# Late routing of the expert stages in a fixed order, with the indices first

## The chip, the cores and the metric

The kernel runs on one core of a Trainium2 chip. The metric is the device time of one execution in microseconds (us). The core has five engines with a queue each, which run their own instructions in order and wait for one another by semaphores: TensorE (PE in the profile, with its weight loads as PEld), VectorE (DVE), ScalarE (ACT), GpSimd (POOL) and SyncE (SP). SP issues most DMA transfers, POOL the indirect ones (gathers and scatters by an index).

## The reference, cut to what matters

A graph network with four layers over 1250 tokens of 512 features. Each layer adds the output of two mixers (a graph part and an attention part), and then that of a mixture of experts:

```python
xn = _layernorm(x, axis=-1)
x = x + _L2_gnn_ref(xn, edge_index, ...) + _L2_mix_ref(xn[None], ...)[0]
x = x + _L2_ffn_ref(_layernorm(x, axis=-1)[None], ...)[0]
...
# the experts, here those of layer 3: every token goes to its 2 best of 8 experts
logits = flat @ gate_w.T
top_vals, top_idx = jax.lax.top_k(logits, TOP_K)
top_w = jax.nn.softmax(top_vals, axis=-1)
combine = jnp.sum(jax.nn.one_hot(top_idx, E, dtype=flat.dtype) * top_w[..., None], axis=1)
out = jnp.zeros_like(flat)
for e in range(E):
    hdn = jax.nn.gelu(flat @ w1[e] + b1[e])
    out = out + combine[:, e:e + 1] * (hdn @ w2[e] + b2[e])
```

The reference computes all experts for all tokens and weights them. The kernel computes only the chosen pairs.

## The kernel before, in words

Everything is float32 in the products that matter. Tokens stand in ten groups of 125. The eight stages (mixers and experts of layers 0 to 3) follow each other, written as one Python function each (L2566). A scheduler then orders the instructions of each engine: it may draw an instruction ahead of others in the program, except those that `tc.keep_in_program_order` pins, which keep their place among the pinned ones. `Pinned` (L308) is a stand-in for VectorE that pins each instruction issued through it.

In an expert stage the 2500 pairs of token and expert are packed into tiles of 128 slots (`SL`). The first three tiles (`NFIRST`) belong to experts 0, 1 and 2 with fixed numbers; they hold the first 128 pairs of each of these. All others are dynamic: tiles in pairs that share an expert (256 slots) and single ones, and the expert of each is only known when the routing has been computed. A load (`Experts.loads`) is one expert's weights with one or two tiles.

`place` (L313) is the routing. Its early part ranks every pair within its expert (products with a triangle and with ones, L327 to L332), makes `r_ohl`, the one-hot of the slot in the tile, and with a product (L373) the token numbers of the first three tiles: `r_idxf`, and `r_destf`, where their results go. `experts.first_rows` then requests the rows of the first tiles from DRAM (`xg<-rows,r_idxf`, L505). The late part is the function `rest` (L391). It works out how many tiles each expert has, and from that the tile of each pair (`r_slot`, `r_own`, `r_slf`), its one-hot `r_oht` (L428, L429), a second product `r_oht` by `r_ohl` on TensorE (L431, 20 matmuls), from its result the token numbers of the dynamic tiles (`r_idx`, L435), the expert number of each load (`r_exi`, L437 to L450), the destinations (`r_dest`, L451) and the weights of the two choices (`shares`, L453). SP loads each expert number into a register (L483) before it can issue the DMA of that expert's weights. The gathers of dynamic rows on POOL need `r_idx`.

`Experts.each` (L519) drives the tiles: for each load n it fetches ahead (weights and rows of a later load), turns the rows of the next load (four transposes on TensorE and a copy to `xgT`, `by_feature`, L544) and yields the load to the stage's own code, which runs the expert's two or three products and scatters the result `y` to a table in DRAM (L566). In layers 0, 1 and 3 the second product's result goes through an add on VectorE (L560 in `put`). Layer 2 works in three groups of loads: `Group.first` (L2332) runs the first products of a whole group, and `second` and `third` follow later.

What the steps of the prediction touch: `rest` is called in `each` at n == 1 (L522), that is behind the code of tile 0; `turn` (L513) copies tile 0's rows on ScalarE and all others on VectorE (L517). These lines decide it:

```python
517  self.turned.append(by_feature(self.to, self.got[n][2], nc.vector.tensor_copy if n else nc.scalar.copy))
521  if n == 1:
522      self.rest()
```

Of the kernel before, what the change touches and what calls it, by code (L numbers as in the profile page):

```python
# [25 lines left out]
E = 8  # L26
# [9 lines left out]
SL = 128  # L36
# [23 lines left out]
def gps_d4_kernel(ctx: ExitStack, tc: tile.TileContext, a: dict, out: bass.AP):  # L60
# [252 lines left out]
    def place(tmp, n_, choice, experts, soft=True, aside=lambda n: None):  # L313
# [5 lines left out]
            return pool.tile(shape, dt, tag=tag, name=name, bufs=1)  # L319

        v = nc.vector
        m, oh = choice.either, choice.oh
        m1, m2 = choice.best

# [11 lines left out]
        ranks = rank[:, None, :NT, :].to_broadcast([TP, 2, NT, E])  # L336

        def size_of(o, ids):
            v.scalar_tensor_tensor(o, ids, -1.0, ids, op0=OP.mult, op1=OP.max)

        ids = sm("r_ids", [SL, NTI])
        size = sm("r_size", [SL, NTI])
# [1 line left out]
        def destination(name, at):  # L344
            w = at.stop - at.start
            kind = sm(f"{name}k", [SL, w])
            v.tensor_scalar(kind, ids[:, at], 0.0, None, op0=OP.is_lt)
            v.scalar_tensor_tensor(kind, size[:, at], 2.0, kind, op0=OP.mult, op1=OP.add)
            free = sm(f"{name}s", [SL, w])
            v.scalar_tensor_tensor(free, ids[:, at], 0.0, spare[:, at], op0=OP.is_equal, op1=OP.mult)  # L350
            dest = sm(name, [SL, w], I32)
            v.scalar_tensor_tensor(dest, kind, -2.0, free, op0=OP.add, op1=OP.add)
            return dest

        own = sm("r_own", [TP, 2, NT, E])
# [33 lines left out]
        aside(1)  # L389

        def rest():  # L391
            v.scalar_tensor_tensor(n[:, 0, :], n[:, 1, :], -2.0, n[:, 0, :], op0=OP.mult, op1=OP.add)
            pm = sm("r_pm", [TP, 2, E, E])
            v.tensor_tensor(pm, uptos, n[:, :, None, :].to_broadcast([TP, 2, E, E]), op=OP.mult)
            end = sm("r_end", [TP, 2, E])
            v.tensor_reduce(end, pm, AX.X, OP.add)
            base = sm("r_base", [TP, 1])
            v.tensor_scalar(base, end[:, 1, E - 1:E], 2.0 * NPAIR * SL, None, op0=OP.max)

            q = sm("r_q", [TP, 3, E])  # L400
            v.tensor_scalar(q[:, 1, :], n[:, 1, :], 2.0 * SL, None, op0=OP.mult)
            v.scalar_tensor_tensor(q[:, 0, :], n[:, 1, :], -2.0 * SL, end[:, 1, :], op0=OP.mult, op1=OP.add)
            v.scalar_tensor_tensor(q[:, 2, :], n[:, 0, :], -1.0 * SL, end[:, 0, :], op0=OP.mult, op1=OP.add)
            v.scalar_tensor_tensor(q[:, 2, :], q[:, 2, :], base, end[:, 1, :], op0=OP.add, op1=OP.subtract)
# [5 lines left out]
            v.tensor_tensor(single, kept[:, :NT, :], q_(1), op=OP.is_ge)  # L410
            slot = sm("r_slot", [TP, NT, E])
            v.tensor_tensor(slot, kept[:, :NT, :], q_(0), op=OP.add)
            late = sm("r_late", [TP, 2, NT, E])
            v.scalar_tensor_tensor(late, kept[:, None, :NT, :].to_broadcast([TP, 2, NT, E]), 0.0, oh, op0=OP.is_ge, op1=OP.mult)
            v.tensor_tensor(single, single, q_(2), op=OP.mult)
            v.tensor_tensor(slot, slot, single, op=OP.add)
            own = sm("r_own", [TP, 2, NT, E])
            v.scalar_tensor_tensor(own, slot[:, None, :, :].to_broadcast([TP, 2, NT, E]), float(SL), late,
                                   op0=OP.add, op1=OP.mult)
            slf = sm("r_slf", [TP, 2 * NT])  # L420
            v.tensor_reduce(slf, own.rearrange("p k t e -> p (k t) e"), AX.X, OP.add)
            sl = sm("r_sl", [TP, 2 * NT], I32)
            v.tensor_copy(sl, slf)
            v.tensor_scalar(sl, sl, 7, None, op0=OP.logical_shift_right)
            slf = sm("r_slf", [TP, 2 * NT])
            v.tensor_copy(slf, sl)
            oht = sm("r_oht", [TP, 2 * NT, NREST], F16)
            v.tensor_tensor(oht, bc(slf, NREST), lanes[:, None, 1:NREST + 1].to_broadcast([TP, 2 * NT, NREST]), op=OP.is_equal)  # L428
            v.tensor_tensor(oht, oht, bc(tokid, NREST), op=OP.mult)  # L429
            ps = bank()  # L430
            mm(ps[:, :NREST], [(ohl[:, j, :], oht[:, j, :]) for j in range(2 * NT)])  # L431
            idx = sm("r_idx", [SL, NREST], I32)
            v.tensor_copy(ids[:, NFIRST:], ps[:, :NREST])
            size_of(size[:, NFIRST:], ids[:, NFIRST:])
            v.tensor_scalar(idx, size[:, NFIRST:], 1.0, 1.0, op0=OP.max, op1=OP.subtract)  # L435

            th = sm("r_th", [1, 2, E])  # L437
            v.tensor_scalar(th[:, 0, :], end[:1, 0, :], base[:1, :], None, op0=OP.add)
            v.tensor_copy(th[:, 1, :], end[:1, 1, :])
            le2 = sm("r_le2", [1, NLOAD, 2 * E])  # L440
            v.tensor_tensor(le2, bc(loadi, 2 * E), th.rearrange("p k e -> p (k e)")[:, None, :]
                            .to_broadcast([1, NLOAD, 2 * E]), op=OP.is_ge)
            ex = sm("r_ex", [1, NLOAD])
            v.tensor_reduce(ex, le2, AX.X, OP.add)
            ge = sm("r_ge", [1, NLOAD])
            v.tensor_scalar(ge, loadi, base[:1, :], -float(E), op0=OP.is_ge, op1=OP.mult)
            v.tensor_tensor(ex, ex, ge, op=OP.add)
            exi = sm("r_exi", [1, NLOAD + 1], I32)
            v.tensor_scalar(exi[:, :NLOAD], ex, float(E - 1), None, op0=OP.min)
            v.tensor_scalar(exi[:, NLOAD:], end[:1, 0, E - 1:E], base[:1, :], 1.0 / SL, op0=OP.add, op1=OP.mult)  # L450
# [7 lines left out]
    class Experts:  # L458


        def __init__(self, pool, rows, weights, rare, ahead=2, bufs=6):

            often = NLOAD - rare
            self.loads = ([(e - NFIRST, (e,)) for e in range(NFIRST)]
                          + [(i, tuple(NFIRST + t for t in tiles)) for k in range(NPAIR)
                             for i, tiles in ((k, (2 * k, 2 * k + 1)), (NPAIR + k, (2 * NPAIR + k,))) if i < often]
                          + [(k, (NFIRST + NPAIR + k,)) for k in range(2 * NPAIR, NLOAD) if k < often]
                          + [(k, (NFIRST + NPAIR + k,)) for k in range(often, NLOAD)])
            self.common = often + NPAIR
            self.often = often + NFIRST  # L470
            soon["rare"] = soon.get("rare", 0) + 1
            self.label = f"rare{soon['rare']}"
            self.pool, self.rows = pool, rows
            self.weights, self.ahead, self.bufs = weights, ahead, bufs
            self.got, self.turned = [], []
            self.ready, self.behind = [], []
            self.most = self.often
            self.fresh = lambda: None

# [15 lines left out]
        def fetch(self):  # L495
# [2 lines left out]
                return  # L498
            i, tiles = self.loads[n]
            w = self.ready[n] if n < len(self.ready) else self.weights(self.expert(i), n)  # L500
            xg = []
            for t in tiles:
                g = self.pool.tile([SL, D], F32, tag="xg", name="xg", bufs=self.bufs)
                at = self.idxf[:, t:t + 1] if t < NFIRST else self.idx[:, t - NFIRST:t - NFIRST + 1]
                nc.gpsimd.indirect_dma_start(g, None, self.rows, bass.IndirectOffsetOnAxis(ap=at, axis=0))  # L505
                xg.append(g)
            self.got.append((tiles, w, xg))

        def start(self):
            for _ in range(self.ahead):  # L510
# [1761 lines left out]
    def layer2_ffn():  # L2272
# [4 lines left out]
        with tc.tile_pool(name="l2o", bufs=1) as op, tc.tile_pool(name="l2b", bufs=1) as bp:  # L2277
# [25 lines left out]

            rows, choice = arrival[2].rows, arrival[2].end()
            experts = Experts(op, rows, weights1, 7)
            experts.fresh = lambda: (half1.fresh(), half3.fresh())
            experts.first_weights()
            place(bp, 1, choice, experts)
            with tc.tile_pool(name="l2e", bufs=1) as pool:
# [13 lines left out]
                class Group:  # L2323
# [8 lines left out]
                    def first(self, source):  # L2332
# [277 lines left out]
```

## Time and profile before

| | us |
|---|---|
| median of 3 runs (2908.19 to 2909.71) | 2908.22 |
| the profiled execution | 2900.07 |
| its span | 2898.4 |
| TensorE busy | 2699.3 (93%) |
| VectorE busy | 1540.1 (53%) |
| ScalarE busy | 787.0 (27%) |
| GpSimd busy | 630.7 (22%) |
| mean granted TensorE clock, of full | 0.966 |

The four expert stages begin, by the first gather with `r_idxf`, at 1300.96 (layer 0), 1751.04 (layer 1), 2403.29 (layer 2) and 2755.98 us (layer 3) of the span. The profiled execution is a single one, with its own time, and sums over its rows are made against that time. Idle time of an engine that nothing waits for costs nothing.

### The profile page before, as it was taken

The numbers are of one execution on the slowest core, as the hardware profiler recorded it, in microseconds if no ns is written. First come the engines' busy times: TensorE is split into PE (matmuls) and PEld (weight loads), VectorE is DVE, ScalarE is ACT, GpSimd is POOL, SyncE is SP. The second block draws the span as 40 slices with busy tenths as digits, with TensorE's granted clock in tenths as the row PEclk, the third lists the DMA queues.
The fourth block names the chain that finished last, engine by engine and source line by source line (L and its number), as shares of the span: only waits on it lengthen the run. The fifth ranks groups of instructions, "written<-read, shape, count | busy, mean of one in ns | idle before, by whom it ended". The sixth has DMA issues, their size and how long they took to land. (4 is left out here: it accounts for less than half of the span.)

```text
span 2898.4 us, 34891 instructions
## 1 busy us (share of the span) xinstructions
PE 2699.3 (93%) x12500; PEld 1924.9 (66%) x12500; DVE 1540.1 (53%) x3845; ACT 787.0 (27%) x1770; POOL 630.7 (22%) x474
## 2 busy tenths in 40 slices
PE   7999999999999999989999998999799998989984
PEld 4457778874577788755457566888654776645663
DVE  6935677674356677553635553334434376443533
ACT  3232333342333444221220452111132123421010
POOL 2444444444100110025101012111000003202141
PEclk9999999999999999999999998999899998999997
DMA  8511112221000651437650018666350016662286
GB/s 233 127 16 16 4 16 45 48 34 16 16 15 1 142 119 53 103 87 230 191 134 14 30 57 302 244 241 232 119 137 30 16 42 208 198 168 77 66 288 229
DMA packets 240092, 314.63 MB, mean 109 GB/s; under 512 B 94689, under 2 KB 136229, under 8 KB 239893
## 3 DMA queue, kind: packets, MB, share of 16 engines
q1 hardware_dynamic: 150156, 236.37, 26.9%
q0 software_dynamic: 86656, 66.90, 9.7%
q10 hardware_dynamic: 3080, 8.81, 1.0%
q8 instruction: 111, 1.82, 0.3%
q14 instruction: 89, 0.72, 0.1%
HBM read 267.80 MB, written 43.86 MB: 108 GB/s over the span
## 5 line engine op out<-in xcount | busy, mean ns | idle before, releaser
L771 POOL DMA_INDIRECT adj<-count,cell x160 | 322.7, 2017 | 375.1 <-DMA adj<-count,cell 329.9
L197 PE MATMUL ps<-xnT,w 128*128 128x500 f32 (+1 forms) x736 | 275.3, 529 | 0.6 <-DVE xnT L941 0.6
L197 PE MATMUL ps<-w,xnT 128*125 128x512 f32 x560 | 252.1, 599 | 0.6 <-ACT xnT L1837 0.6
L197 PE MATMUL ps<-xgT,w 128*128 128x256 f32 (+1 forms) x1344 | 237.0, 335 | 4.7 <-ACT xgT L551 2.1
L197 PEld LDWEIGHTS ps<-xgT,w 128*128 128x128 f32 x1344 | 212.2, 195 | 42.0 <-issue 15.4
L197 PEld LDWEIGHTS ps<-xnT,w 128*128 128x128 f32 x736 | 139.5, 193 | 122.7 <-issue 116.2
L197 PEld LDWEIGHTS ps<-w,xnT 128*125 128x125 f32 x560 | 102.3, 190 | 114.6 <-issue 113.1
L1334 PE MATMUL ps<-w,hT 128*125 128x256 f32 (+1 forms) x704 | 171.2, 379 | 0.5 <-ACT p L1339 0.5
L1339 ACT COPY p<-ps 125x256 f32<-125x256 f32 (+5 forms) x272 | 93.6, 351 | 265.5 <-PE ps L1334 245.7
L1334 PEld LDWEIGHTS ps<-w,hT 128*125 128x125 f32 (+1 forms) x704 | 130.3, 188 | 19.0 <-ACT p L1339 0.9
L551 DVE COPY xgT<-ps 128x512 f32<-128x512 f32 x90 | 59.7, 687 | 143.7 <-PE ps L550 112.5
L566 POOL DMA_INDIRECT table<-y,r_dest x82 | 85.6, 1044 | 228.8 <-DVE y L2066 124.8
L197 PE MATMUL ps<-w,hT 128*128 128x512 f32 (+1 forms) x272 | 124.7, 595 | 3.6 <-issue 2.3
L223 DVE TENSOR_TENSOR xn<-ps,xn 125x256 f32<-125x256 f32 (+1 forms) x180 | 80.2, 450 | 78.7 <-PE ps L197 54.6
L2050 ACT ACTIVATE hT<-ps,b 128x256 f32<-128x256 f32 (+1 forms) x120 | 50.5, 424 | 236.7 <-PE ps L197 225.9
L1334 PE MATMUL ps<-t,sh 128*125 128x256 f32 (+1 forms) x480 | 112.6, 379 | 0.0
L505 POOL DMA_INDIRECT xg<-rows,r_idx x82 | 79.1, 965 | 152.1 <-PE ps L550 122.5
L197 PE MATMUL ps<-hs,AT 125*125 125x512 f32 x400 | 101.6, 410 | 4.9 <-PEq L902 3.3
L1334 PEld LDWEIGHTS ps<-t,sh 128*125 128x125 f32 (+1 forms) x480 | 89.9, 188 | 12.8
L197 PE MATMUL ps<-AT,part 125*128 125x500 f32 (+1 forms) x480 | 92.6, 355 | 0.0
L197 PEld LDWEIGHTS ps<-hs,AT 125*125 125x125 f32 x400 | 75.2, 191 | 24.6 <-issue 4.6
L197 PEld LDWEIGHTS ps<-AT,part 125*128 125x128 f32 x480 | 79.3, 189 | 13.4 <-issue 1.0
(520 smaller groups left out, 5032.3 us busy)
## 6 DMA issues: line engine op xcount, KB each, us to landing
w<-in_L_ffn_we_dram SPq DMA_DIRECT2D x58, 1024.0 KB
w<-in_L_ffn_w_dram SPq DMA_DIRECT2D x62, 512.0 KB
came<-table SPq DMA_DIRECT2D x40, 448.0 KB
w<-in_L_mix_W_dram SPq DMA_DIRECT2D x16, 1024.0 KB
w<-in_L_ffn_w_dram SPq DMA_DIRECT2D x47, 256.0 KB
AT<-adj SPq DMA_DIRECT2D x10, 1093.8 KB
AT<-adj SPq DMA_DIRECT2D x20, 546.9 KB
rows<-z SPq DMA_DIRECT2D x40, 224.0 KB
```

The costliest lines, as they stand in the source:

```text
L197: nc.tensor.matmul(o, l, r, start=(i == 0), stop=(i == n - 1))
L223: nc.vector.tensor_tensor(dst, ps, dst, op=OP.add)
L505: nc.gpsimd.indirect_dma_start(g, None, self.rows, bass.IndirectOffsetOnAxis(ap=at, axis=0))
L551: copied(xgT[:, :, j * SL:(j + 1) * SL], ps.rearrange("p (c s) -> p c s", c=NC))
L566: d = nc.gpsimd.indirect_dma_start(to, bass.IndirectOffsetOnAxis(ap=at, axis=0), y, None)
L771: nc.gpsimd.indirect_dma_start(adj, bass.IndirectOffsetOnAxis(ap=self.cell[:, c:c + 1], axis=0), self.count[:, c:c + 1], None, compute_op= ...
L1334: nc.tensor.matmul(banks[b], ls(k), rs(k), start=first and k == 0, stop=k == nk - 1, skip_group_check=True)
L1339: nc.scalar.copy(o, banks[b])
L2050: nc.scalar.activation(hT[f // NC][:, f % NC, :ns], ps[:, :ns], AF.Gelu, bias=b1[:, f:f + 1])
```

## The change

`place` gets a `Pinned()` of its own, and all instructions of `rest`, `size_of` and `destination` are issued through it, so that they stand on VectorE in the order of the program, which has the indices ahead of the expert numbers and the destinations. `Experts` gets `found`, which runs `rest` and requests the rows of the first dynamic load; layer 2 calls it in its first group, behind the turning of tile 1 and ahead of tile 0's product. Where `found` ran, `each` does not call `rest` again, and `fetch` takes the rows that were asked for. In layer 2 `still` is 3, so the rows of the first three tiles are copied on ScalarE; elsewhere it is 1, as before. Layers 0, 1 and 3 call `rest` where they did.

```diff
+        pinned = Pinned()
...
         def size_of(o, ids):
-            v.scalar_tensor_tensor(o, ids, -1.0, ids, op0=OP.mult, op1=OP.max)
+            pinned.scalar_tensor_tensor(o, ids, -1.0, ids, op0=OP.mult, op1=OP.max)
...
         def rest():
-            v.scalar_tensor_tensor(n[:, 0, :], n[:, 1, :], -2.0, n[:, 0, :], op0=OP.mult, op1=OP.add)
+            pinned.scalar_tensor_tensor(n[:, 0, :], n[:, 1, :], -2.0, n[:, 0, :], op0=OP.mult, op1=OP.add)
...
-            v.tensor_tensor(oht, oht, bc(tokid, NREST), op=OP.mult)
+            pinned.tensor_tensor(oht, oht, bc(tokid, NREST), op=OP.mult)
             ps = bank()
             mm(ps[:, :NREST], [(ohl[:, j, :], oht[:, j, :]) for j in range(2 * NT)])
             idx = sm("r_idx", [SL, NREST], I32)
-            v.tensor_copy(ids[:, NFIRST:], ps[:, :NREST])
+            pinned.tensor_copy(ids[:, NFIRST:], ps[:, :NREST])
...
-            self.ready, self.behind = [], []
+            self.ready, self.behind, self.asked, self.still = [], [], {}, 1
...
             w = self.ready[n] if n < len(self.ready) else self.weights(self.expert(i), n)
+            self.got.append((tiles, w, self.asked.get(n) or self.ask(tiles)))
+
+        def ask(self, tiles):
             xg = []
             for t in tiles:
                 g = self.pool.tile([SL, D], F32, tag="xg", name="xg", bufs=self.bufs)
                 at = self.idxf[:, t:t + 1] if t < NFIRST else self.idx[:, t - NFIRST:t - NFIRST + 1]
                 nc.gpsimd.indirect_dma_start(g, None, self.rows, bass.IndirectOffsetOnAxis(ap=at, axis=0))
                 xg.append(g)
-            self.got.append((tiles, w, xg))
+            return xg
+
+        def found(self):
+
+            if not self.asked:
+                self.rest()
+                self.asked[NFIRST] = self.ask(self.loads[NFIRST][1])
...
-                self.turned.append(by_feature(self.to, self.got[n][2], nc.vector.tensor_copy if n else nc.scalar.copy))
+                self.turned.append(by_feature(self.to, self.got[n][2], nc.vector.tensor_copy if n >= self.still else nc.scalar.copy))
...
-                if n == 1:
+                if n == 1 and not self.asked:
                     self.rest()
...
+            experts.still = NFIRST
...
                             experts.turn()
+                            experts.found()
```

More of the change, by code (lines that the diff above doesn't have):

```diff
@@ L346, in destination @@
             kind = sm(f"{name}k", [SL, w])
-            v.tensor_scalar(kind, ids[:, at], 0.0, None, op0=OP.is_lt)
-            v.scalar_tensor_tensor(kind, size[:, at], 2.0, kind, op0=OP.mult, op1=OP.add)
+            pinned.tensor_scalar(kind, ids[:, at], 0.0, None, op0=OP.is_lt)
+            pinned.scalar_tensor_tensor(kind, size[:, at], 2.0, kind, op0=OP.mult, op1=OP.add)
             free = sm(f"{name}s", [SL, w])
-            v.scalar_tensor_tensor(free, ids[:, at], 0.0, spare[:, at], op0=OP.is_equal, op1=OP.mult)
+            pinned.scalar_tensor_tensor(free, ids[:, at], 0.0, spare[:, at], op0=OP.is_equal, op1=OP.mult)
             dest = sm(name, [SL, w], I32)
-            v.scalar_tensor_tensor(dest, kind, -2.0, free, op0=OP.add, op1=OP.add)
+            pinned.scalar_tensor_tensor(dest, kind, -2.0, free, op0=OP.add, op1=OP.add)
             return dest
@@ L391, in rest @@
         def rest():
-            v.scalar_tensor_tensor(n[:, 0, :], n[:, 1, :], -2.0, n[:, 0, :], op0=OP.mult, op1=OP.add)
+            pinned.scalar_tensor_tensor(n[:, 0, :], n[:, 1, :], -2.0, n[:, 0, :], op0=OP.mult, op1=OP.add)
             pm = sm("r_pm", [TP, 2, E, E])
-            v.tensor_tensor(pm, uptos, n[:, :, None, :].to_broadcast([TP, 2, E, E]), op=OP.mult)
+            pinned.tensor_tensor(pm, uptos, n[:, :, None, :].to_broadcast([TP, 2, E, E]), op=OP.mult)
             end = sm("r_end", [TP, 2, E])
-            v.tensor_reduce(end, pm, AX.X, OP.add)
+            pinned.tensor_reduce(end, pm, AX.X, OP.add)
             base = sm("r_base", [TP, 1])
-            v.tensor_scalar(base, end[:, 1, E - 1:E], 2.0 * NPAIR * SL, None, op0=OP.max)
+            pinned.tensor_scalar(base, end[:, 1, E - 1:E], 2.0 * NPAIR * SL, None, op0=OP.max)
             q = sm("r_q", [TP, 3, E])
[L401 to L404, printed above, removed]
+            pinned.tensor_scalar(q[:, 1, :], n[:, 1, :], 2.0 * SL, None, op0=OP.mult)
+            pinned.scalar_tensor_tensor(q[:, 0, :], n[:, 1, :], -2.0 * SL, end[:, 1, :], op0=OP.mult, op1=OP.add)
+            pinned.scalar_tensor_tensor(q[:, 2, :], n[:, 0, :], -1.0 * SL, end[:, 0, :], op0=OP.mult, op1=OP.add)
+            pinned.scalar_tensor_tensor(q[:, 2, :], q[:, 2, :], base, end[:, 1, :], op0=OP.add, op1=OP.subtract)
             def q_(k):
@@ L409, in rest @@
             single = sm("r_single", [TP, NT, E])
-            v.tensor_tensor(single, kept[:, :NT, :], q_(1), op=OP.is_ge)
+            pinned.tensor_tensor(single, kept[:, :NT, :], q_(1), op=OP.is_ge)
             slot = sm("r_slot", [TP, NT, E])
-            v.tensor_tensor(slot, kept[:, :NT, :], q_(0), op=OP.add)
+            pinned.tensor_tensor(slot, kept[:, :NT, :], q_(0), op=OP.add)
             late = sm("r_late", [TP, 2, NT, E])
-            v.scalar_tensor_tensor(late, kept[:, None, :NT, :].to_broadcast([TP, 2, NT, E]), 0.0, oh, op0=OP.is_ge, op1=OP.mult)
@@ L415, in rest @@
-            v.tensor_tensor(single, single, q_(2), op=OP.mult)
-            v.tensor_tensor(slot, slot, single, op=OP.add)
+            pinned.scalar_tensor_tensor(late, kept[:, None, :NT, :].to_broadcast([TP, 2, NT, E]), 0.0, oh, op0=OP.is_ge, op1=OP.mult)
+            pinned.tensor_tensor(single, single, q_(2), op=OP.mult)
+            pinned.tensor_tensor(slot, slot, single, op=OP.add)
             own = sm("r_own", [TP, 2, NT, E])
-            v.scalar_tensor_tensor(own, slot[:, None, :, :].to_broadcast([TP, 2, NT, E]), float(SL), late,
+            pinned.scalar_tensor_tensor(own, slot[:, None, :, :].to_broadcast([TP, 2, NT, E]), float(SL), late,
@@ L419, in rest @@
                                    op0=OP.add, op1=OP.mult)
             slf = sm("r_slf", [TP, 2 * NT])
-            v.tensor_reduce(slf, own.rearrange("p k t e -> p (k t) e"), AX.X, OP.add)
+            pinned.tensor_reduce(slf, own.rearrange("p k t e -> p (k t) e"), AX.X, OP.add)
             sl = sm("r_sl", [TP, 2 * NT], I32)
-            v.tensor_copy(sl, slf)
-            v.tensor_scalar(sl, sl, 7, None, op0=OP.logical_shift_right)
+            pinned.tensor_copy(sl, slf)
+            pinned.tensor_scalar(sl, sl, 7, None, op0=OP.logical_shift_right)
@@ L425, in rest @@
             slf = sm("r_slf", [TP, 2 * NT])
-            v.tensor_copy(slf, sl)
+            pinned.tensor_copy(slf, sl)
             oht = sm("r_oht", [TP, 2 * NT, NREST], F16)
-            v.tensor_tensor(oht, bc(slf, NREST), lanes[:, None, 1:NREST + 1].to_broadcast([TP, 2 * NT, NREST]), op=OP.is_equal)
-            v.tensor_tensor(oht, oht, bc(tokid, NREST), op=OP.mult)
+            pinned.tensor_tensor(oht, bc(slf, NREST), lanes[:, None, 1:NREST + 1].to_broadcast([TP, 2 * NT, NREST]), op=OP.is_equal)
@@ L432, in rest @@
             idx = sm("r_idx", [SL, NREST], I32)
-            v.tensor_copy(ids[:, NFIRST:], ps[:, :NREST])
+            pinned.tensor_copy(ids[:, NFIRST:], ps[:, :NREST])
             size_of(size[:, NFIRST:], ids[:, NFIRST:])
-            v.tensor_scalar(idx, size[:, NFIRST:], 1.0, 1.0, op0=OP.max, op1=OP.subtract)
+            pinned.tensor_scalar(idx, size[:, NFIRST:], 1.0, 1.0, op0=OP.max, op1=OP.subtract)
             th = sm("r_th", [1, 2, E])
-            v.tensor_scalar(th[:, 0, :], end[:1, 0, :], base[:1, :], None, op0=OP.add)
-            v.tensor_copy(th[:, 1, :], end[:1, 1, :])
+            pinned.tensor_scalar(th[:, 0, :], end[:1, 0, :], base[:1, :], None, op0=OP.add)
+            pinned.tensor_copy(th[:, 1, :], end[:1, 1, :])
             le2 = sm("r_le2", [1, NLOAD, 2 * E])
-            v.tensor_tensor(le2, bc(loadi, 2 * E), th.rearrange("p k e -> p (k e)")[:, None, :]
+            pinned.tensor_tensor(le2, bc(loadi, 2 * E), th.rearrange("p k e -> p (k e)")[:, None, :]
                             .to_broadcast([1, NLOAD, 2 * E]), op=OP.is_ge)
             ex = sm("r_ex", [1, NLOAD])
-            v.tensor_reduce(ex, le2, AX.X, OP.add)
+            pinned.tensor_reduce(ex, le2, AX.X, OP.add)
             ge = sm("r_ge", [1, NLOAD])
-            v.tensor_scalar(ge, loadi, base[:1, :], -float(E), op0=OP.is_ge, op1=OP.mult)
-            v.tensor_tensor(ex, ex, ge, op=OP.add)
+            pinned.tensor_scalar(ge, loadi, base[:1, :], -float(E), op0=OP.is_ge, op1=OP.mult)
+            pinned.tensor_tensor(ex, ex, ge, op=OP.add)
             exi = sm("r_exi", [1, NLOAD + 1], I32)
-            v.tensor_scalar(exi[:, :NLOAD], ex, float(E - 1), None, op0=OP.min)
-            v.tensor_scalar(exi[:, NLOAD:], end[:1, 0, E - 1:E], base[:1, :], 1.0 / SL, op0=OP.add, op1=OP.mult)
+            pinned.tensor_scalar(exi[:, :NLOAD], ex, float(E - 1), None, op0=OP.min)
+            pinned.tensor_scalar(exi[:, NLOAD:], end[:1, 0, E - 1:E], base[:1, :], 1.0 / SL, op0=OP.add, op1=OP.mult)
             soon["to"] = table[n_], destf, destination("r_dest", slice(NFIRST, NTI)), soon["to"][3]
```

## The prediction

> **What bounds the kernel now.** I read the page first.
>
> ```profile
> span 2898.4 us, 34891 instructions
> PE 2699.3 (93%) x12500; PEld 1924.9 (66%) x12500; DVE 1540.1 (53%) x3845; ACT 787.0 (27%) x1770; POOL 630.7 (22%) x474
> ```
>
> TensorE (PE) is busy 93% of the span, so what matters is whether the change opens or closes a hole on PE. The late routing runs once in each of four expert stages. I then read the timeline around each, and the table of PE's waits for the layer-1 stage from 1784 to 2045 us, which holds no row: PE has no slack there. Timeline rows are start, duration, engine, instruction, count, and in brackets the idle time before it and its releaser. Layer 1:
>
> ```profile
> 1756.35 0.72 DVE L429 TENSOR_TENSOR r_oht<-r_oht,tokid 125x540 f16<-125x540 f16 x1
> 1757.49 1.11 PE L550 MATMUL ps<-ident,xg 128*128 128x128 f32 x4 [7.35 <-DMA xg<-rows,r_idxf]
> 1759.40 10.28 PE L197 MATMUL ps<-xgT,w 128*128 128x128 f32 x64 [0.80 <-ACT xgT L551]
> 1776.82 0.66 PE L197 MATMUL ps<-r_oht,r_ohl 125*128 125x27 f16 x20
> 1777.02 0.69 DVE L560 TENSOR_TENSOR y<-ps,erow 128x512 f32<-128x512 f32 x1 [6.18 <-PE ps L197]
> 1777.33 7.39 PE L197 MATMUL ps<-xgT,w 128*128 128x128 f32 x64
> ```
>
> The reader sees that VectorE finishes `r_oht` at 1757.07, before tile 0 has even started, in time in which PE waits for rows. The routing product on PE (the fourth row) comes 20 us later and waits for nothing. The third and sixth rows are the same 64 matmuls: after the 7 us hole they took 2.89 us more. Layer 3:
>
> ```profile
> 2755.81 0.16 DVE L392 SCALAR_TENSOR_TENSOR r_n<-r_n 125x8 f32<-125x8 f32 x1
> 2760.70 0.72 DVE L429 TENSOR_TENSOR r_oht<-r_oht,tokid 125x540 f16<-125x540 f16 x1
> 2767.33 0.66 PE L197 MATMUL ps<-r_oht,r_ohl 125*128 125x27 f16 x20
> 2767.53 0.69 DVE L560 TENSOR_TENSOR y<-ps,erow 128x512 f32<-128x512 f32 x1 [1.03 <-PE ps L197]
> 2772.06 2.05 PE L197 MATMUL ps<-xgT,w 128*128 128x128 f32 x16 [0.89 <-DVE xgT L551]
> 2775.98 1.31 PE L550 MATMUL ps<-ident,xg 128*128 128x128 f32 x8 [1.00 <-DMA xg<-rows,r_idx]
> ```
>
> The same picture, with about 1.9 us of holes on PE behind it. Layer 0 and layer 2:
>
> ```profile
> 1317.01 0.66 PE L197 MATMUL ps<-r_oht,r_ohl 125*128 125x27 f16 x20
> 1317.21 0.69 DVE L560 TENSOR_TENSOR y<-ps,erow 128x512 f32<-128x512 f32 x1 [1.85 <-PE ps L197]
> 1319.50 0.99 POOL L505 DMA_INDIRECT xg<-rows,r_idx  x1 [0.30 <-DVE ws L311]
> 1325.13 2.09 PE L550 MATMUL ps<-ident,xg 128*128 128x128 f32 x8 [2.60 <-issue]
> ...
> 2408.16 1.12 PE L550 MATMUL ps<-ident,xg 128*128 128x128 f32 x4 [0.38 <-DMA xg<-rows,r_idxf]
> 2411.66 0.67 PE L197 MATMUL ps<-r_oht,r_ohl 125*128 125x27 f16 x20
> 2413.31 0.95 POOL L505 DMA_INDIRECT xg<-rows,r_idx  x1 [6.51 <-DVE r_destk L348]
> 2416.79 0.66 PE L550 MATMUL ps<-ident,xg 128*128 128x128 f32 x4 [2.25 <-DMA xg<-rows,r_idx]
> 2419.39 1.08 PE L550 MATMUL ps<-ident,xg 128*128 128x128 f32 x4 [1.95 <-DMA xg<-rows,r_idx]
> ```
>
> In layer 2 PE stands 2.25 + 1.95 = 4.2 us for the first dynamic rows.
>
> **The change, part by part.**
>
> *Fixed order, layers 0, 1, 3.* `rest()` is called at n == 1, behind tile 0's use. The scheduler had drawn its instructions ahead of that; pinned, they may not pass. In the built program VectorE's order becomes: tile 1's copy, tile 0's add `y` (L560), then the whole of `rest()`. PE's order keeps the `r_oht` product directly behind tile 0's second product and ahead of tile 1's first, and PE takes its matmuls in order. So the add waits for PE, `rest()` waits for the add, and PE waits for `rest()`: cover that was free (VectorE was idle 13 us in layer 1) is given away.
>
> Length of that wait: in layer 3 `rest()` took 2755.81 to 2761.42 = 5.61 us up to `r_oht`. Of this the eight expert-number instructions (L438 to L450), now behind the indices, held 1.48 us of start-to-start time; `r_q`, `r_single`, `r_late`, which had run earlier, add 0.51 us; some six pairs that now depend on their neighbour start about 0.12 us later each (0.16 us instructions start 0.20 apart when dependent, 0.08 when not): 5.61 - 1.48 + 0.51 + 0.7 = 5.3 us (4.6 to 5.9). The add ends 0.69 + 0.20 us after the product's old start, so PE stands 6.2 us in each of the three layers.
>
> Clock after the hole. The table of stretches (us, busy time and count of PE, PEld, DVE, ACT, POOL, then PE's granted clock, DMA share, GB/s) has, behind layer 3's hole that ended at 2759.45:
>
> ```profile
> 2760.00:2764.00 4.00, 3.33 (x16) 2.92 (x15) 1.39 (x2) 1.20 (x2) 0.00 (x0) 0.50 0.26 73
> ```
>
> PE runs there at half its clock. Restarting cost 2.89 us in layer 1 (10.28 against 7.39) and 1.74 + 0.37 = 2.1 us in layer 3 (16 matmuls 3.79 against 2.05, four transposes 0.97 against 0.60). After a 6.2 us hole I take 2.5 us in layer 1 and 2.1 in layer 3; the bounds are 0 and 3.4 us. The Trainium skill (TensorE: Matmul & The Clock Gate, section What's actually happening) says that one idle window of about 3.4 us halves the clock and that one busy window restores it; by that alone a restart would lose an estimated 1.7 us, and my total would be about 1 us lower. The row's 2.89 us is more than one such window, so the measurement decides.
>
> - Layer 1: no slack, 6.2 + 2.5 = **+8.7** (6.2 to 9.6). Its next dynamic weights are issued at 1781.26, when tile 1 frees a buffer, which moves too; the later expert numbers (about 1786) cost nothing more.
> - Layer 3: 6.2 + 2.1 - 1.9 of old holes, which the stall swallows, = **+6.4** (4.3 to 9). The rows are requested about 5.5 us later and arrive before PE needs them. ScalarE now does tile 1's second activation before the shares' exponential, so tile 1's second product is no longer split around tile 2's; I price that inside the 1.9.
> - Layer 0: PE needed 1317.01 to 1322.53 = 5.5 us from the product to the rows' first transposes: 1323.2 + 5.5 = 1328.7, with 2 us of slow clock 1330.7; the rows, requested at about 1324.8, take the old 5.6 us: 1330.4. So 1330.7 instead of 1325.13, less the slow stretch that followed the old hole (transposes 2.09 against 1.04, eight matmuls 2.61 against 1.85; I expect half of 1.8 us back): **+4.7** (2.1 to 7). Four POOL multiplications of the next stage's weights (L1615, 6.20 us) move behind six gathers and scatters; PE has shared products there, so I put it at nothing, at most 1 us either way.
>
> *Weights.* The expert numbers come about 2 us after the indices; SP's value loads wait for them with all later loads behind. In layer 2 the first load followed the numbers by 1.1 us, so in layer 3 I get about 2778.3 for weights used at 2780.43 + 6.4 = 2786.8: 8.5 us for 1.25 MB, 3.4 us at the 364 GB/s that the stretch 2772 to 2776 moved. Covered; if not, up to 2 us per layer.
>
> *Layer 2.* `found()` runs `rest()` before tile 0's product, and VectorE no longer stops for the copies. Its `r_oht` would end at about 2408.4; the product starts when tile 1's transposes end, 2409.28 instead of 2411.66. At the low clock it takes some 0.4 us longer, so the rows go out 2.0 us earlier. They arrive into emptier DMA queues, since the weights now come behind them. Tiles 1 and 2 cost ScalarE two copies of 0.59 us, between a 1.28 us table load and an activation that waits for PE anyway. I take **-2.3**; at best the whole 4.2 goes, at worst later weights or ScalarE eat all and 1 us more.
>
> Sum: 4.7 + 8.7 + 6.4 - 2.3 = **+17.5 us**. The profiled execution took 2900.07 us (span 2898.4 and 1.7 around it), 0.28% under the median of 2908.22; it becomes 2917.6, and the median **2925.7 us** (+0.6%).
>
> **Rivals.**
>
> - *Short stalls.* The clock recovers at once and layer 2 wins all its holes: 3.8 + 6.2 + 4.3 - 4.2 = +10: 2918 us. For: PE's short holes in layer 0 cost one slow stretch only. Against: the 2.89 us row.
> - *Late weights.* Expert numbers behind the indices make the first dynamic product wait in layers 0, 2 and 3 as well, 2 us each: +23.5: 2932 us. For: DMA moved 340 to 360 GB/s in these stretches. Against: the 8.5 us of room.
> - *Faster.* Indices first shorten the path to the first dynamic rows, and their waits close: 2.6 in layer 0, 4.2 in layer 2, 1.9 in layer 3, together -8.7: 2899.5 us. It decides if `r_oht` is ready when tile 0's second product ends (1317.0, 1776.8, 2767.3). Against: the add that `rest()` now stands behind cannot start before that moment.
> - *Nothing.* Stalls fall into holes that are there anyway: 2908. Only layers 0 and 3 have such holes, 2.6 and 1.9 us against 6.2.
>
> **How the numbers follow.** Forecast 0.74, short stalls 0.10, late weights 0.08, faster 0.05, nothing 0.03. A change under 0.2% (5.8 us) can't be told from none here. Slower is the first three: 0.92. The range goes from a little under short stalls to a little over late weights: 2916 to 2935.
>
> **What would show it.** After: `r_oht` (L429's successor) starts behind the L560 add in layers 0, 1, 3; the first `r_oht` matmul of each shows some 6 us idle, released by VectorE; the granted clock drops to 0.50 behind it; layer 1 stays without other waits and its stage grows by 8 to 9 us; in layer 2 the waits for `xg<-rows,r_idx` shrink from 4.2 to about 2 us. I am wrong if PE does not stand at `r_oht`, or if the stage from layer 1's routing to its end grows by under 5 us.

## The result, and the profile after

The changed kernel takes 2927.09 us (median of 5 runs, 2923.12 to 2937.05) against 2908.19 us for the kernel before on the same chip. The ratio is 1.0075, 95% interval 1.0057 to 1.0093: about 22 us slower (17 to 27); the two medians alone differ by 18.9. The profiled execution took 2926.65 us, close to its median; the one of before, 2900.07, was 8 us under its own. So the two spans differ by 26.6 us, and I compare stage by stage. In the profile after, lines have moved: every pinned instruction of the routing is now L311 (the `Pinned` stand-in), the transposes and copies of `by_feature` are L560 and L561, the add of `put` is L570, the gathers L509.

The first lines of the page, after:

```profile
span 2925.0 us, 34891 instructions
PE 2710.2 (93%) x12500; PEld 1931.7 (66%) x12500; DVE 1543.6 (53%) x3843; ACT 787.2 (27%) x1772; POOL 628.0 (21%) x474
```

The same matmuls, 10.9 us more of them: a slower clock somewhere (the mean granted clock is 0.962, before 0.966). The rest of the difference is idle time. The timeline of layer 1 shows both (columns: start, duration, engine, instruction, count, and in brackets the idle time before it with its releaser):

```profile
1780.56 0.60 PE L560 MATMUL ps<-ident,xg 128*128 128x128 f32 x4
1781.00 7.03 PE L197 MATMUL ps<-w,hT 128*128 128x512 f32 x16
1788.07 0.69 DVE L570 TENSOR_TENSOR y<-ps,erow 128x512 f32<-128x512 f32 x1 [6.18 <-PE ps L197]
1788.67 0.16 DVE L311 SCALAR_TENSOR_TENSOR r_n<-r_n 125x8 f32<-125x8 f32 x1
1793.27 0.72 DVE L311 TENSOR_TENSOR r_oht<-r_oht,tokid 125x540 f16<-125x540 f16 x1
1794.04 0.69 PE L197 MATMUL ps<-r_oht,r_ohl 125*128 125x27 f16 x20 [6.01 <-DVE r_oht L311]
1794.58 9.51 PE L197 MATMUL ps<-xgT,w 128*128 128x128 f32 x64
```

VectorE sat idle for 6.18 us until tile 0's add could run, and only then began the late routing (`r_n`), which took 1788.67 to 1793.99 = 5.32 us up to `r_oht`. TensorE stood 6.01 us. The 64 matmuls behind took 9.51 us; before, they took 7.39. The view of the tile `r_oht` sums the stalls up; its answer for the kernel before has no such line:

```profile
its engine sat idle before it (us, times) until:
  DVE r_oht L311: 18.0, 3
```

Three stalls, 18.0 us: layers 0, 1 and 3. Layer 0 and, 37 and 58 us later in the same stage, two more rows:

```profile
1325.74 0.69 PE L197 MATMUL ps<-r_oht,r_ohl 125*128 125x27 f16 x20 [6.00 <-DVE r_oht L311]
...
1362.59 6.19 POOL L1625 TENSOR_SCALAR w<-w,nw 128x512 f32<-128x512 f32 x4 [6.84 <-DMA w<-in_L_mix_w_qkv_dram]
...
1383.64 3.78 PE L197 MATMUL ps<-w,hT 128*128 128x512 f32 x4 [5.16 <-issue]
```

POOL now stands 13 us (6.84 + 6.19) at the multiplications of a weight, in the middle of the gathers and scatters of the stage, and a hole of 5.16 us opens on TensorE 80 us behind the stage's start (before: 8.5 us on POOL, and 1.79 us at the corresponding place). Layer 2, where the change does something else:

```profile
2427.52 0.72 DVE L311 TENSOR_TENSOR r_oht<-r_oht,tokid 125x540 f16<-125x540 f16 x1
2428.70 0.74 PE L197 MATMUL ps<-r_oht,r_ohl 125*128 125x27 f16 x20
2430.36 0.94 POOL L509 DMA_INDIRECT xg<-rows,r_idx  x1 [3.85 <-DVE r_th L311]
2435.38 0.63 PE L560 MATMUL ps<-ident,xg 128*128 128x128 f32 x4 [0.93 <-DMA xg<-rows,r_idx]
2438.01 0.63 PE L560 MATMUL ps<-ident,xg 128*128 128x128 f32 x4 [0.27 <-DMA xg<-rows,r_idx]
```

The product waits for nothing, and the waits for the first dynamic rows fell from 4.2 to 0.93 + 0.27 = 1.2 us. Layer 3, on TensorE:

```profile
2789.76 0.69 PE L197 MATMUL ps<-r_oht,r_ohl 125*128 125x27 f16 x20 [6.00 <-DVE r_oht L311]
2790.30 3.76 PE L197 MATMUL ps<-xgT,w 128*128 128x128 f32 x16
2798.72 1.04 PE L560 MATMUL ps<-ident,xg 128*128 128x128 f32 x8
2801.73 3.01 PE L197 MATMUL ps<-w,hT 128*128 128x512 f32 x4 [1.98 <-ACT hT L2563]
```

Behind the stall the 16 matmuls again run at the low clock (3.76 against 2.03), the first dynamic rows are there without a wait, and a further wait of 1.98 us for an activation follows.

The table gives each stage's length in the profiled executions, from one stage's first gather with `r_idxf` to the next one's (layer 3: to the end of the span); the kernels of the experiments are in it for later. Where a kernel leaves a stage as before, the lengths agree within 0.6 us in layer 1, 1.3 in layer 2, 3.0 in layer 3 and 3.6 in layer 0 (four of its six within 0.2). The first 1300 us, which no kernel touches, vary by 13 us from one execution to another: that is what makes spans poor evidence here.

| kernel | layer 0 | layer 1 | layer 2 | layer 3 | ratio to before |
|---|---|---|---|---|---|
| before | 450.1 | 652.2 | 352.7 | 142.4 | |
| after | 460.3 | 659.2 | 349.1 | 153.0 | 1.0075 (1.0057 to 1.0093) |
| l2_only | 450.2 | 652.2 | 350.2 | 143.2 | 0.9988 (0.9977 to 1.0000) |
| pin_l1 | 450.2 | 659.2 | 353.0 | 142.7 | 1.0024 (1.0011 to 1.0036) |
| pin_l3 | 450.2 | 652.4 | 353.7 | 151.2 | 1.0020 (1.0009 to 1.0030) |
| pin_l0 | 464.9 | 651.8 | 352.7 | 143.5 | 1.0023 (1.0011 to 1.0034) |
| pin_l1_busy | 453.1 | 656.9 | 353.1 | 141.9 | 1.0021 (1.0005 to 1.0036) |
| l0_late | 458.1 | 651.9 | 352.4 | 143.4 | 1.0026 (1.0012 to 1.0039) |
| numbers_first | 460.5 | 659.6 | 349.8 | 150.5 | 1.0073 (1.0047 to 1.0099) |
| l2_vec | 449.5 | 652.2 | 357.8 | 140.5 | 1.0006 (0.9994 to 1.0018) |
| early | 449.9 | 649.7 | 349.5 | 140.0 | 0.9965 (0.9951 to 0.9978) |
| early_loose | 446.0 | 649.9 | 350.2 | 138.4 | 0.9955 (0.9939 to 0.9971) |
| early_late | 444.3 | 650.5 | 347.8 | 138.2 | 0.9963 (0.9948 to 0.9978) |

### The profile page after: what moved, and what is told of

It is laid out like the page before. It is cut to its first block, busy times and chain, and to the rows that moved or that the text cites. A ratio compares the mean times of both kernels' runs of the same rounds, so it can differ in the third digit from the quotient of the medians.

```text
span 2925.0 us, 34891 instructions
## 1 busy us (share of the span) xinstructions
PE 2710.2 (93%) x12500; PEld 1931.7 (66%) x12500; DVE 1543.6 (53%) x3843; ACT 787.2 (27%) x1772; POOL 628.0 (21%) x474
## 5 line engine op out<-in xcount | busy, mean ns | idle before, releaser
L561 DVE COPY xgT<-ps 128x512 f32<-128x512 f32 x88 | 58.4, 687 | 150.2 <-PE ps L560 121.9
L509 POOL DMA_INDIRECT xg<-rows,r_idx x82 | 78.8, 961 | 168.0 <-PE ps L560 125.2
```

Of the source, the lines that this page charges most:

```text
L561: copied(xgT[:, :, j * SL:(j + 1) * SL], ps.rearrange("p (c s) -> p c s", c=NC))
```

## The experiments

**One layer at a time.** The first four kernels take the change apart by layer. `n_` is the number that `place` is given: 3 for layer 0, 0 for layer 1, 1 for layer 2, 2 for layer 3.

l2_only, from the changed kernel:

```diff
         v = nc.vector
-        pinned = Pinned()
+        pinned = Pinned() if n_ == 1 else nc.vector
```

> The fixed order only in layer 2, with its early product, its early request and its copies on ScalarE; layers 0, 1 and 3 issue the late routing unpinned, as before. Theory (the loss is the three stalls at the r_oht product, layer 2 is a gain): no PE wait at r_oht in layers 0, 1 and 3, layer 2 keeps its 3.6 us, so 3 to 4 us faster than before (ratio 0.9986 to 0.9990). Rival (the indices ahead of the expert numbers, or the copies on ScalarE, cost something themselves, and the 3.6 us of layer 2 is variation between two profiles): 0 to 5 us slower than before.

Measured: 0.9988 (0.9977 to 1.0000), 3.5 us faster, with an interval that just reaches no change. No wait at `r_oht` anywhere; layer 2's stage is 2.4 us shorter than in the profile of before, and TensorE waits for no dynamic rows. By the profile it is as the theory had it: the indices first, the early request and the copies on ScalarE are a gain where the routing stands ahead of the products.

pin_l1, pin_l3 and pin_l0 take away layer 2's part and pin one other layer:

```diff
         v = nc.vector
-        pinned = Pinned()
+        pinned = Pinned() if n_ == 0 else nc.vector    # 2 in pin_l3, 3 in pin_l0
...
-            experts.still = NFIRST
...
-                            experts.found()
```

> The fixed order only in layer 1; layer 2 and the others as before. Theory: one stall of 6.0 us at r_oht on PE and a restart of the clock, 6.9 (stage difference of the two profiles) to 8.7 us (predicted) slower than before, ratio 1.0024 to 1.0030; layer 1's stage longer by as much, the others unchanged. Rival (PE has slack later in the stage or in the next mixers): under 4 us slower.

> The fixed order only in layer 3. Theory: stall of 6.0 us, restart of the clock, and a wait of some 2 us for the activation hT behind it that the prediction did not have; 8 to 10.5 us slower than before, ratio 1.0028 to 1.0036. Rival (the prediction's sizes are right and the rest of the 10.5 us between the two profiles is variation of the tail): 6.4 us slower, ratio 1.0022.

> The fixed order only in layer 0. Theory: 4.7 us at the stall and the first dynamic rows, as predicted, and some 5 us more from a second hole on PE 80 us behind the stage's start, because the four multiplications w by nw on POOL now stand behind more gathers and wait there for their load: 10 us slower, ratio 1.0034, and the second hole is there. Rival (the second hole belongs to one profile and not to the order): 4.7 us slower, ratio 1.0016, and no hole there that the kernel before lacks.

Measured, layer 1: 1.0024, 7.0 us; its stage 659.2, 6.9 us longer than before and the same as in the full change. Theory right.

Layer 3: the profile shows the wait of 6.00 us and behind it 2.48 us for `hT`, and the stage is 8.8 us longer. Up to the last pair of transposes, 100 us into the stage, the shift is 8.0 us (102.26 against 94.28 before; 92.52 to 94.37 in the six other kernels that leave layer 3 as before; 102.92 in the full change): what comes on top of that is the tail behind the last tile, which varies by 2 us from execution to execution anyway. The times give 1.0020, 5.8 us (2.6 to 8.7), which does not tell theory from rival; the profile speaks for the theory's size.

Layer 0: the times give 1.0023, 6.7 us (3.2 to 9.9). The profiled execution is the longest of that kernel's eleven (2910.84 to 2927.62), and its stage is 14.8 us longer. In it POOL and TensorE read:

```profile
1374.10 6.19 POOL L1625 TENSOR_SCALAR w<-w,nw 128x512 f32<-128x512 f32 x4 [8.86 <-DMA w<-in_L_mix_w_qkv_dram]
```

```profile
1335.12 0.69 PE L197 MATMUL ps<-r_oht,r_ohl 125*128 125x27 f16 x20 [6.00 <-DVE r_oht L311]
...
1393.72 1.16 PE L197 MATMUL ps<-xgT,w 128*128 128x128 f32 x8 [2.53 <-issue]
1400.88 2.08 PE L197 MATMUL ps<-w,hT 128*128 128x512 f32 x2 [5.13 <-ACT hT L1694]
```

So the second hole is not in one execution alone: it is in the full change, here and in no profile where layer 0 is as before (longest in that part of the stage 3.3 us). But it does not come with the order alone: numbers_first, below, has the same fixed order in layer 0, with other instructions first, and no wait over 3.1 us there. Nor do the rows show how POOL would make it. At its end three engines go on at once in pin_l0:

```profile
1400.46 0.37 ACT L1694 ACTIVATE hT<-ps,b 128x128 f32<-128x128 f32 x1 [11.31 <-remote]
1400.47 1.29 DVE L561 COPY xgT<-ps 128x512 f32<-128x512 f32 x2 [4.59 <-remote]
1400.71 0.99 POOL L509 DMA_INDIRECT xg<-rows,r_idx  x1 [2.54 <-remote]
```

`remote` is an update of a semaphore for which the profile finds no instruction. Here all three wait for TensorE's semaphore, and the activation needs the eight matmuls that the row above ends at 1394.88, 5.6 us earlier (ends of matmuls are modelled, so the rows do not tell whether the matmuls or only the update came late). The same three engines go on so at 1383.11 to 1384.76 in the full change, and in l2_only, pin_l1, pin_l3 and pin_l1_busy, which leave layer 0 as before, at the end of their longest holes there, 2.8 to 3.3 us. The expert stages of l2_vec, early_loose and early_late, all taken on another chip than the rest of the experiments, have no such row. Whether POOL's wait lengthens this, or what else does, is not shown. How much of it a typical execution pays is less than this profile suggests, since the median is only 6.7 us up and the stall by itself is 5.8 (below).

The four parts add up to 7.0 + 5.8 + 6.7 - 3.5 = 16.0 us by times, just under the lower end of the change's 17 to 27.

**The clock.** pin_l1_busy gives TensorE something to do during the wait of layer 1, behind tile 0's second product:

```diff
                             put(pool, ps, t, b2, 4)
+                            if t == 0:
+                                mm(bank(), [(hT[1][:, NC - 1, :SL], w2[1][:, NC - 1, :])] * 7)
```

> The fixed order only in layer 1, and behind tile 0's second product seven more products of 128x512 whose result nobody reads, so that TensorE works during the wait for r_oht (8 such took 2 x 3.0 us, so some 5.3 of the 6.0 us). It computes more than is needed, and the output stays. Theory (the low clock behind the stall costs 2.3 to 2.9 us beside the 6.0 us of the wait): the wait at r_oht shrinks to about 0.7 us, no half-rate stretch follows, and layer 1's stage is 4.0 to 4.7 us longer than before instead of 6.9. Rival (the clock's restart costs nothing of its own, all is the wait): 6.9 us as without the products, ratio 1.0024.

Measured: layer 1's stage 656.9, 4.6 us longer than before where pin_l1 is 6.9. (The ratio, 1.0021, can't separate 2 us; layer 0, which the edit doesn't touch, was 3 us longer in this execution.) The stretches of pin_l1 around the wait, and then of pin_l1_busy (columns: stretch, its length, busy time and count of PE, PEld, DVE, ACT, POOL, then PE's granted clock, DMA share, GB/s):

```profile
1790.00:1794.00 4.00, 0.00 (x0) 0.00 (x0) 3.68 (x13) 0.00 (x0) 0.53 (x1) 0.76 0.86 304
1794.00:1798.00 4.00, 4.00 (x36) 4.00 (x36) 2.99 (x17) 0.37 (x1) 1.91 (x2) 0.50 0.15 33
1798.00:1802.00 4.00, 4.00 (x34) 4.00 (x34) 0.76 (x5) 3.60 (x6) 1.89 (x2) 0.89 0.71 201
```

```profile
1784.00:1788.00 4.00, 4.00 (x10) 1.62 (x9) 3.69 (x14) 0.00 (x0) 0.70 (x1) 1.00 0.16 66
1788.00:1792.00 4.00, 4.00 (x50) 3.82 (x49) 2.98 (x17) 1.08 (x3) 1.91 (x2) 1.00 0.55 188
```

Both kernels wait for the same `r_oht`, one idle and one at work. The granted clock stays at 1.00 in the second. The 64 matmuls behind, in the timelines of pin_l1 and of pin_l1_busy:

```profile
1794.00 0.69 PE L197 MATMUL ps<-r_oht,r_ohl 125*128 125x27 f16 x20 [6.00 <-DVE r_oht L311]
1794.54 9.47 PE L197 MATMUL ps<-xgT,w 128*128 128x128 f32 x64
```

```profile
1788.18 0.66 PE L197 MATMUL ps<-r_oht,r_ohl 125*128 125x27 f16 x20
1788.69 7.39 PE L197 MATMUL ps<-xgT,w 128*128 128x128 f32 x64
```

9.47 - 7.39 = 2.1 us is what the restart of the clock costs in layer 1, apart from the wait. The rival of a clock that recovers at once has fallen.

**Layer 0's second hole.** l0_late is pin_l0 with the four multiplications held back by a gain that depends on the 11th load's activation (times zero, so that the value stays):

```diff
+                nw = norm_gain()
...
                         nc.scalar.activation(hT[:, :ns], ps[:, :ns], AF.Relu, bias=b1)
+                        soon["at"] = soon.get("at", 0) + 1
+                        if soon["at"] == 11:
+                            gain2 = S.small.tile([P, NC], F32, tag="gain2", name="gain2", bufs=1)
+                            nc.vector.scalar_tensor_tensor(gain2, hT[:, :NC], 0.0, nw, op0=OP.mult, op1=OP.add)
+                            soon["gain2"] = gain2
...
-                    nw = norm_gain()
...
-                    soon["L1"] = [normed_w(k, nw) for k in (2, 1)] + [load_w(a["L1_mix_w_out"])]
+                    soon["L1"] = [normed_w(2, nw), normed_w(1, soon["gain2"])] + [load_w(a["L1_mix_w_out"])]
```

> The fixed order only in layer 0, and the four multiplications w by nw on POOL made to depend on the 11th load's activation, so that they stand behind nearly all gathers and scatters of the stage. Theory (the hole of 5 us on PE some 80 us behind the stage's start comes from POOL, which waits 7 to 9 us for that weight with gathers and scatters queued behind): no such hole, layer 0's stage 4 to 6 us longer than before instead of 10 to 15. Rival (the hole has another cause, as late weights on SP's queue): hole and stage as in the run with the fixed order only in layer 0, 14.8 us longer.

Measured in the profile: no hole over 3.0 us behind the stall, the stage 8.0 us longer than before instead of 14.8, somewhat more than the 4 to 6 expected. At the single tile 50 us into the stage, which is ahead of the second hole, the shift is 5.76 us in the full change (50.37 against 44.61), 5.85 in pin_l0 and 5.78 in l0_late: that is the price of the stall. But the times do not follow: 1.0026 (1.0012 to 1.0039) against 1.0023 for pin_l0. That POOL's wait makes the hole fits these two profiles, but l0_late's longest wait, 2.98 us, ends with the same `remote` rows; that its removal saves time is not shown.

**Indices first, or expert numbers first.** numbers_first is the changed kernel with the block of `r_th` to `r_exi` moved ahead of `r_q`, still pinned:

```diff
+            th = sm("r_th", [1, 2, E])
...
+            pinned.tensor_scalar(exi[:, NLOAD:], end[:1, 0, E - 1:E], base[:1, :], 1.0 / SL, op0=OP.add, op1=OP.mult)
             q = sm("r_q", [TP, 3, E])
```

> The changed kernel with the expert numbers ahead of the indices in the fixed order. Theory (the place of the late routing behind tile 0's add costs, and each instruction ahead of r_oht lengthens the wait): the three waits at r_oht grow from 6.0 to about 7.5 us, layer 2 gives back some 1.5 us; about 6 us slower than the changed kernel, ratio to before about 1.0095. Rival (late expert numbers and with them late weights are part of the loss): as fast as the changed kernel or faster, ratio at most 1.0075.

Measured: 1.0073 (1.0047 to 1.0099), which holds both numbers. The three waits grew, by 2 us each and not by 1.5, and layer 2 has one of 1.10 us. TensorE in layer 1, in numbers_first:

```profile
1794.60 0.69 PE L197 MATMUL ps<-r_oht,r_ohl 125*128 125x27 f16 x20 [7.97 <-DVE r_oht L311]
```

Yet the stage is only 0.5 us longer than in the full change (659.6 against 659.2), since the clock came back sooner behind the longer wait (granted 0.62 and then 1.00 in the two stretches of 4 us behind its end, 0.50 and 0.87 in the full change): from the product to tile 2's transposes it took 8.95 us, 9.89 in the full change and 7.74 before. Late weights are not what was saved: in the full change TensorE's waits for the experts' weights come to one of 0.4 us, in layer 2, and in layer 1 the next dynamic weights are issued 37.6 us into the stage in the full change and 39.5 in numbers_first, although the numbers were there 4 and 12 us earlier. In layer 0 the single tile 50 us into the stage comes 9.4 us late instead of 5.8, and yet the two stages are equally long: the second hole is missing. POOL was through with its multiplications 53 us into the stage instead of 65. The theory's length of the wait is right in kind, its price per microsecond is not.

**The copies on ScalarE.** l2_vec is l2_only without them:

```diff
-            experts.still = NFIRST
```

> The fixed order only in layer 2, with its early product and early request, but without the copies on ScalarE: tile 1's rows are copied on VectorE again, and that copy stands in VectorE's order ahead of the late routing. Theory (whatever the routing is queued behind on VectorE is paid on TensorE): the copy ends about 0.9 us behind tile 1's transposes, the routing takes 5.3 us, so TensorE waits some 6 us at r_oht in layer 2 as well; the gain of 3.3 us turns into a loss of 2 to 4 us, ratio to before 1.0007 to 1.0014. Rival (the gain comes from the early request alone, the copies are indifferent): 3 us faster than before, ratio 0.999.

Measured: 1.0006 (0.9994 to 1.0018), not to be told from before; in the profile layer 2's stage is 357.8, 5.1 us longer than before. In layer 2 of l2_vec:

```profile
2412.66 1.12 PE L560 MATMUL ps<-ident,xg 128*128 128x128 f32 x4 [0.52 <-DMA xg<-rows,r_idxf]
2419.79 0.71 PE L197 MATMUL ps<-r_oht,r_ohl 125*128 125x27 f16 x20 [6.01 <-DVE r_oht L311]
```

One copy of tile 1's rows ahead of the routing on VectorE, and the same stall is there in layer 2. By the profile the early product without the copies on ScalarE gains nothing: the copies must get out of its way. (The intervals of l2_vec and l2_only still overlap.)

**The routing moved ahead.** early keeps the order of the change and calls `rest` of layers 0, 1 and 3 behind the turning of tile 0's rows, ahead of its first product:

```diff
             for n in range(first, last):
-                if n == 1 and not self.asked:
-                    self.rest()
                 self.fetch()
                 if n == len(self.turned):
                     self.turn()
+                if n == 0 and self.still == 1:
+                    self.rest()
```

> The changed kernel with the late routing of layers 0, 1 and 3 called ahead of tile 0's first product, behind the turning of its rows, instead of behind tile 0; order fixed as in the change. Theory (not the fixed order but its place costs): no wait at r_oht over 1 us, the rows of the first dynamic tiles come early, and with layer 2's gain 3 to 8 us faster than before, ratio 0.997 to 0.999. Rival (a fixed order costs by itself, as it holds other work of VectorE back): 3 us or more slower than before.

Measured: 0.9965 (0.9951 to 0.9978), 10 us faster than before. Layer 1 of early on TensorE:

```profile
1763.07 1.12 PE L560 MATMUL ps<-ident,xg 128*128 128x128 f32 x4 [7.22 <-DMA xg<-rows,r_idxf]
1763.98 0.74 PE L197 MATMUL ps<-r_oht,r_ohl 125*128 125x27 f16 x20
1764.98 8.94 PE L197 MATMUL ps<-xgT,w 128*128 128x128 f32 x64 [0.26 <-ACT xgT L561]
```

The product falls into the 0.8 us in which TensorE waited for tile 0's copy anyway; only layer 3 waits 1.02 us for `r_oht`. With the fixed order kept and its place changed, layers 1 and 3 turn from a loss into a gain of some 2.5 us each, layer 2 keeps its gain, and layer 0 ends as before. In layer 0, tile by tile, early is 4.3 us ahead of before 40 us into the stage (40.31 against 44.61 at the same transposes) and loses it in a hole of 4.86 us 67 us into the stage; there too POOL had stood at the multiplications (7.13 us of waiting for the weight), and there too the copy that TensorE waits for was released by `remote`.

early_loose pins layer 2 alone, early_late adds l0_late's edit to early:

```diff
         v = nc.vector
-        pinned = Pinned()
+        pinned = Pinned() if n_ == 1 else nc.vector
```

> As the run with the late routing early in all layers, but pinned in layer 2 alone: in layers 0, 1 and 3 it is issued unpinned, so that the scheduler may again put the expert numbers ahead of the indices. Theory (the place of the product on TensorE decides, the order within the routing only by its length): layers 0 and 1 as with the fixed order, in layer 3 some 1.5 us more of waiting at r_oht; 6 to 8 us faster than before, ratio 0.9973 to 0.998. Rival (the fixed order with the indices first is what makes the early routing fast): within 3 us of before.

> The late routing early in all layers, in fixed order, and the four multiplications w by nw on POOL behind the 11th load of layer 0. In the run without the second part, layer 0 was 4.3 us ahead of before 40 us into the stage and lost it in a hole of 4.9 us at 67 us. Theory (POOL, held by the wait for that weight, makes this hole): the hole goes, layer 0's stage is 3 to 4 us shorter than before, all in all 11 to 13 us faster than before, ratio 0.9955 to 0.9962. Rival (the hole has another cause): as without it, ratio 0.9965.

Measured: early_loose 0.9955 (0.9939 to 0.9971), early_late 0.9963 (0.9948 to 0.9978). Pinning is not needed for the gain: without it, layer 3 waits 0.9 us at `r_oht`, not 1.5 more. In early_late no wait over 1.5 us is left between 60 and 90 us into layer 0, and its stage is 5.8 us shorter than before, early's 0.2. That cannot be put down to the edit: early_loose, on the same chip and without it, has POOL at the multiplications for 13.6 us, no wait over 2.4 us there and a stage 4.1 us shorter than before; early was taken on another chip. Again the times of the three do not differ beyond their intervals, so which of them is best stays open; all three beat both kernels.

## Why the prediction was right, and where it was not

Predicted were 2925.7 us (2916 to 2935) and slower; measured 2927.09. The direction and the main mechanism were right; that the median came within 1.4 us is partly luck, since the terms of layers 0 and 3 were too small, that of layer 1 too large, and the change itself measures 17 to 27 us where 17.5 were forecast. By its steps:

- **The wait.** "PE stands 6.2 us in each of the three layers" from a chain of 5.3 us: 6.00, 6.01 and 6.00 us, chain 5.32. Right, and the mechanism is shown by l2_only and early (no routing behind the add, no wait) and by pin_l1.
- **The clock.** 2.5 us in layer 1, measured 2.1 by pin_l1_busy; 2.1 in layer 3, measured 3.76 - 2.03 = 1.7 for the 16 matmuls and 1.06 - 0.60 = 0.5 for the transposes; the granted clock reads 0.50 behind both waits. The restart differs by place: 1.2 us behind the wait of 8.0 us in numbers_first. The Trainium skill's rule (TensorE: Matmul & The Clock Gate, section What's actually happening) gave an estimated 1.7 us; these measurements lie on both sides of it. The page also says that the window is free-running and that the moment of recovery depends on where in it the work starts; that fits 2.1 and 1.2, and no run here shifts the phase by itself.
- **Layer 1, +8.7.** The stage grew by 6.9. The stall and the restart cost 8.3 us between tile 1's and tile 2's transposes (40.15 - 16.78 = 23.37 us, before 33.52 - 18.48 = 15.04). What the working left out is a gain ahead of the stall: tile 1's transposes come 1.7 us sooner (16.78 against 18.48 us into the stage). Tile 0's rows land 0.5 us sooner, and its first product runs less of its time at the low clock.
- **Layer 3, +6.4.** 8.0 (pin_l3) to 8.6 us (full change) at the last pair. The step that failed is "- 1.9 of old holes, which the stall swallows": the rows did come in time, but a wait of 2.0 to 2.5 us for `hT` stood in the place of the old holes. It is also in early (1.98 us), where TensorE stands only 1.02 us at `r_oht`, so the stall of 6 us is not its cause. In the full change ScalarE's table load had ended 4.0 us before that activation, which then starts at 2801.31 together with VectorE (2801.47) and POOL (2801.71), all three released by `remote` as in layer 0's second hole. early_late, with the same layer 3 on another chip, has neither the wait nor these rows. The cause stays open.
- **Layer 0, +4.7.** The stall cost 5.8 us at 50 us into the stage, within the 2.1 to 7 given. Not in the sum is the second hole. The multiplications on POOL were put "at nothing, at most 1 us either way", because TensorE had shared products there. Before, POOL was through at 1344.3 and the last shared product of the stage ended at 1363.9; after, at 1368.8 and 1371.3: what POOL had put off then fell into time without cover. The other profiles fit that: POOL is through 19 to 20 us ahead of the last shared product in numbers_first and where layer 0 is as before, and 15 us in early_loose, and TensorE's longest wait behind it is 1.2 to 3.3 us; it is through 7 us ahead in early, 2.5 in the full change and 0.5 in pin_l0, with waits of 4.9, 5.2 and 5.1. But the `remote` rows leave it open whether POOL is the cause, so whether this term failed is not shown. The profile of the full change loses 4.7 us more by 100 us into the stage, pin_l0's 8.2 more. In the times of pin_l0 it is at most a few microseconds.
- **Weights.** "Covered": right, TensorE waited 0.4 us for one of them.
- **Layer 2, -2.3.** -3.6 between the two profiles, -2.4 in l2_only, and 3.5 us by l2_only's times. The row waits went from 4.2 to 1.2, a little further than the 2 predicted.

In sum the profile's stages grew by 10.2 + 6.9 - 3.6 + 10.5 = 24.0 us where 17.5 were predicted; 2.5 more lie ahead of any change. The ratio's interval, 17 to 27 us, holds both. Of the rivals, the short stalls fell with pin_l1_busy and late weights with the wait tables. The faster one's condition, `r_oht` ready when tile 0's second product ends, is met in early, and there the kernel is faster, by 10 us where that rival had 8.7.

## What to carry to other kernels

An instruction pinned in an in-order queue waits for everything that stands ahead of it, and what it feeds on another in-order engine waits with it: before fixing an order, look up what the scheduler had drawn ahead and which idle time it used. Here the same order cost 7 us in a layer when it stood behind one add and saved 2.5 us in the same layer when it stood ahead of it. Where work is delayed, look also at what other queues do half a stage later: the cover that hid a wait there may have ended, though no run here shows that it cost time.

## What was not expected of the hardware

The price of an idle stretch of TensorE is not proportional to it: 6.0 us of waiting cost 8.3 us at tile 2, and in numbers_first 8.0 us cost only 0.9 more, because the clock returned after 1.2 instead of 2.1 us of loss.

With VectorE idle instead of working at the routing, tile 0's rows in layer 1 landed sooner: TensorE's wait for them was 6.75 to 7.00 us in the four kernels that held the routing back, 7.22 to 8.05 in the nine others. In the same stage the third gather's issue on POOL took 0.95 us instead of 1.37. The profile of before, and of after:

```profile
1753.69 1.37 POOL L505 DMA_INDIRECT xg<-rows,r_idxf  x1 [0.30 <-issue]
```

```profile
1766.41 0.95 POOL L509 DMA_INDIRECT xg<-rows,r_idxf  x1 [0.30 <-issue]
```

The Trainium skill (SBUF — State Buffer, section SBUF: two separate sides) says that while some VectorE instructions run, GpSimd is locked out of a shared port and cannot write the descriptors of its transfers. That would agree with these rows, but no run separates it from other causes, and in early and early_late the third issue took 0.99 and 1.01 us with waits of 7.22 and 7.38.
